# One VectorE instruction per pair of tiles for the moments, biases as a constant last column, one gelu per block, 23 squarings, and idle products of TensorE inside a planned schedule of an SSM, delta-rule and expert stack

## The chip, the cores and the metric

The kernel runs on one core of a Trainium2 chip. The metric is the device time of one launch in microseconds (us): 726.42 us, the median of 3 runs of the kernel before (725.71 to 728.25). All data is float32.

## What is computed

The input is `u`, 8 sequences of 512 steps with 128 features. Four layers follow each other; each normalises its input over the features (no gain, eps 1e-5) and adds its result to the stream. Cut to what matters:

```python
def layernorm(x):                              # m, v over the 128 features
    return (x - m) / sqrt(v + 1e-5)

# 1. gated scan. W_in and W_out (128x128) are divided by max(largest singular value, 1)
raw = u @ Wp.T + bp ;  delta, b, c = split(raw, 3)
a = min(exp(-softplus(delta + delta_bias) * alpha), 1 - 1e-4) ;  b, c = tanh(b), tanh(c)
...                                            # a, b, c divided by max(sigma of [[a,b],[0,c]], 1)
z[t+1] = a[t] * z[t] + b[t] * u_scaled[t]      # per feature, along the 512 steps
x = x + (c * z) @ Wout_n.T

# 2. one linear operation of 8, chosen once for all tokens
idx = argmax(log_softmax(logits) + gumbel)
x = x + layernorm(x) @ W[idx] + b[idx]

# 3. delta rule, 16 heads of 8 features, state S (8x8) per head and sequence
q, k, v, beta = split(layernorm2(layernorm(x)) @ w_qkvb + b_qkvb, 4) ;  k = k / |k| ;  beta = sigmoid(beta)
S = S + (beta * (v - S k)) outer k ;  o = S q  # per step
x = x + (layernorm(x) + o @ w_out + b_out)

# 4. top 2 of 8 experts, 128 -> 512 -> 128
p = softmax(xf @ w_router) ;  weights = the two largest of p
x = x + sum over the two experts of weight * (gelu(xf @ w1[e] + b1[e]) @ w2[e] + b2[e])
```

## The kernel before

**Tiles and stages.** The 4096 tokens are 32 tiles of 128 tokens: 16 time steps of the 8 sequences. Tiles come in 8 chunks of 4 (a chunk is `g` in the code), and chunks in groups of 4, 8, 8, 8 and 4 tiles for the experts. For a chunk, `scanned` does layer 1 (feature-major, 128 x 512), `ssm_out` and `linear` layer 1's output and layer 2, `delta_in` prepares queries, keys, values and the small 4 x 4 matrices of layer 3, `delta_rule` runs the recurrence, `route` chooses experts. When a group is complete, `experts` writes its token rows to a table in memory sorted by expert (indirect DMAs of POOL), runs the experts over blocks of 128 rows (15 blocks for 4 tiles, 23 for 8; 99 in all), and gathers the two results of each token back.

**The recurrence.** `delta_rule` goes through the 32 tiles in 4 blocks of 4 steps each: 128 blocks, each a chain of 6 VectorE operations. `so<-kq,st` multiplies keys and queries by the state, `st<-so` sums over the 9 terms, `prod<-tmat,st` and `st<-prod` solve the four steps of the block, `st<-kq,st` forms the state's terms and the second `st<-st` sums them into the next state. The state lives in two PSUM banks used in turn, `st[0]` (`st0`) and `st[1]`: columns 0 to 319 of each bank hold terms, the next 32 the sums `w`, and `st[1]` also holds `u_16`, the results of 16 steps, that ScalarE copies to `upd` once per tile. Columns 352 to 511 of `st[0]` aren't used. TensorE's other products use the banks `in`, `ph` and `po`, two each.

**Front work.** `spectral` finds the largest singular value of both weight matrices: `SQUARINGS + 1` = 25 products of the 128 x 128 matrix by itself, rescaled every third step by sums that TensorE, VectorE and ScalarE compute together; two such chains run interleaved, one per matrix, and end in `gain`, which `ssm_out` needs. `moments` takes for each tile one `bn_stats` and one `bn_aggr` of VectorE; `factors` makes from mean and variance a scale and a shift on POOL, `normalised` applies them on ScalarE. This is done four times in the stream, with the suffixes i, a, b and e.

**Experts.** `hidden_of` loads the weights of a block (`w1b`, 128 x 516 with the bias in the last 4 columns) from `w1b_dram`, a copy of the weights with biases that is made at the start. The row is chosen by a register. Four products fill `ph`, then four gelu instructions of 128 x 128 read it, each with its bias column, and `second` multiplies `hid` by `w_sb`. `linear` adds the chosen bias `bsel` to `x1` on POOL first.

**What sets the order.** Every call on an engine is recorded by `Recorder` in a `Plan` as an operation with a cost (`_cost`), a due time (`nc.key`) and its data dependences; a bank of PSUM may be chosen by the planner. `place` puts them on five engine timelines one after the other, by due time and by the earliest possible start. `best` tries `DRAFTS` = 60 drafts with changed due times and keeps the shortest. `emit` issues the operations in that order, so that each engine's queue has a fixed order. Waits between engines are derived from data and from PSUM banks afterwards. All recorded operations carry one source line, 317, in the profile (325 in the changed kernel), so groups are told apart by names and sizes.

Of the kernel before, what the change touches and what calls it, by code (L numbers as in the profile page):

```python
# [25 lines left out]
SQUARINGS = 24  # L26
# [44 lines left out]
class Plan:  # L71
# [112 lines left out]
    def best(self):  # L184
# [3 lines left out]
        for draft in range(DRAFTS):  # L188
# [10 lines left out]
            for turn in range(ROUNDS + 1):  # L199
# [4 lines left out]
                if kept is None or end < kept[0]:  # L204
                    kept = end, order, index, due, self.switch
        for bank, i in kept[2].items():
            bank.index = i
# [73 lines left out]
    def emit(self):  # L281
        kind = mybir.EngineType
        with self.tc.manual_schedule(engines={kind.PE, kind.DVE, kind.Activation, kind.SP}):
            for op, switch in self.best():
                if switch:
                    self.hw.scalar.preload_act_table_set(switch)  # L286
# [54 lines left out]
def _cost(engine, name, n, kw):  # L341

    if engine == "tensor":
        return 0.2 if name == "transpose" else 0.22 + 0.0019 * max(_size(kw["rhs"])[1] - 96, 0)
# [4 lines left out]
    if engine == "scalar":  # L349
        columns = sum(isinstance(kw.get(k), bass.AP) for k in ("bias", "scale"))  # L350
        return 0.18 + 0.00085 * n + (0.0, 0.0001 * n, 0.13)[columns]
    return 0.22 + 0.0015 * n if n < 64 else 0.4 + 0.0017 * n
# [5 lines left out]
DRAFTS = 60  # L358
# [3 lines left out]
LAG = {"tensor": 0.4, "vector": 0.3, "scalar": 0.3, "gpsimd": 0.3, "sync": 0.3}  # L362
SWITCH = (3.0, 6.0, 9.0, 12.0)
# [3 lines left out]
def seq_kernel(  # L367
# [93 lines left out]
    WIDE = {"both": 2 * N, "xne": P, "w1b": NHB * P + NHB, "drive": N + B, "z": N + B, "kq": NR * QN, "prod": B * BL * BL}  # L461
# [23 lines left out]
    def po_tile():  # L485
        return nc.bank(0, 1, 2)
# [20 lines left out]
    R_BP, R_AL, R_DB, R_G, R_B, R_QKVB, R_B1 = 0, 3, 4, 5, 6, 7, 11  # L507
    n_rows = R_B1 + NE * NHB
# [4 lines left out]
    nc.scalar.dma_start(rows[R_QKVB : R_QKVB + 4], b_qkvb.rearrange("(c p) -> c p", p=P))  # L513
    nc.scalar.dma_start(rows[R_B1:], b1.rearrange("e (c p) -> (e c) p", p=P))
# [12 lines left out]
    nc.sync.dma_start(wr, w_router)  # L527

# [88 lines left out]

    nc.vector.memset(st[0], 0.0)
# [33 lines left out]
    def col(r):  # L652
# [3 lines left out]
    FW = NHB * P + NHB  # L656
    w1b_dram = dram.tile([NE * P, FW], F32, tag="w1b_dram", name="w1b_dram")
    nc.key = 0.0
    nc.sync.dma_start(w1b_dram[:, 0 : NHB * P], w1.rearrange("e d f -> (e d) f"))
    nc.sync.dma_start(  # L660
        w1b_dram[:, NHB * P :].rearrange("(e p) c -> p e c", p=P),
        cols[:, R_B1:].rearrange("p (e c) -> p e c", c=NHB),
    )
# [41 lines left out]
    nc.vector.tensor_copy(w_row, pk[:, 4:5])  # L705
    b_row = ctile([P, 1], "b_row", U32)
    nc.vector.tensor_copy(b_row, topi[:, 0:1])
    wsel = ctile([P, D], "wsel")
    bsel = ctile([P, D], "bsel")
    for dst, src, row in (  # L710
        (wsel, ffn_W.rearrange("e d f -> (e d) f"), w_row),
        (bsel, ffn_b, b_row),
# [6 lines left out]
        )  # L719


    def moments(src, part, bufs=2):

        n = src.shape[1]
        st = stile([P, NT, 6], "st" + part)
# [851 lines left out]
```

## Time and profile before

| what | number |
|---|---|
| median of 3 runs | 726.42 us (725.71 to 728.25) |
| profiled execution, whole | 728.65 us |
| profiled execution, span of the trace | 726.9 us |
| granted TensorE clock, mean of the span | 0.832 |
| instructions | 11166 |
| TensorE (PE) busy | 520.2 us (72%) |
| VectorE (DVE) busy | 527.0 us (73%) |
| ScalarE (ACT) busy | 468.8 us (64%) |
| GpSimd (POOL) busy | 548.1 us (75%) |
| DMA moved | 105.94 MB, mean 146 GB/s |

The busy shares are means over the whole span, and no engine stands out in them; what limits a stage is read from its stretch. The profile's 40 slices give each engine's busy share in tenths, a slice being 18.2 us, and `PEclk` the clock that TensorE was granted in tenths of full speed. In TensorE's rows a float32 product appears as two records, so 792 records of `ph<-xbT,w1b` are the 396 products of 99 blocks. Groups name output and inputs by the program's names: `st` is one of the two state banks, `ph`, `in`, `po` the other banks.

### The profile page before, as it was taken

Reading aid. Unit: us, or ns where it says so; the run is one execution under the profiler, and the core shown is the slowest. Engines: PE = TensorE matmul, PEld = TensorE weight load, DVE = VectorE, ACT = ScalarE, POOL = GpSimd, SP = SyncE. Lnnn points to the kernel's source line nnn. Section 1 sums busy time; section 2 is a strip of 40 time slices with the busy share of each in tenths; the row PEclk is TensorE's granted clock in tenths of the full one; section 3 lists DMA queues with packets and bytes.
Section 4 is the critical chain, followed back from the end, with each engine's and each line's share of the span. In section 5 each row is a group of like instructions: output and inputs, shape, how many; then the busy total and the mean of one; then the engine's idle time right before and its main releaser. Section 6 shows DMA issues by size and latency. Waiting matters only on the chain. (4 is left out here: it accounts for less than half of the span.)

```text
span 726.9 us, 11166 instructions
## 1 busy us (share of the span) xinstructions
PE 520.2 (72%) x2948; PEld 403.9 (56%) x2948; DVE 527.0 (73%) x1468; ACT 468.8 (64%) x1062; POOL 548.1 (75%) x681
## 2 busy tenths in 40 slices
PE   5885466576584288699558788883978887988890
PEld 4672124435353156368326577662857776888890
DVE  5775068998999799999959999995798998230013
ACT  3865747654692679998675987852675743675560
POOL 6667485694768899699868998978478878876454
PEclk9856566877699599889758889996899999999995
DMA  3734263233352564276456456565686786569662
GB/s 106 200 108 123 60 148 79 73 95 88 78 125 75 143 178 125 76 181 179 127 148 162 111 138 169 163 173 135 168 211 184 201 245 194 171 192 276 168 176 80
DMA packets 97717, 105.94 MB, mean 146 GB/s; under 512 B 9100, under 2 KB 72535, under 8 KB 97655
## 3 DMA queue, kind: packets, MB, share of 16 engines
q1 hardware_dynamic: 92992, 96.66, 49.2%
q0 software_dynamic: 4160, 8.53, 4.0%
q8 instruction: 25, 0.41, 0.3%
q14 instruction: 38, 0.30, 0.1%
q10 hardware_dynamic: 502, 0.03, 0.0%
HBM read 81.26 MB, written 23.94 MB: 145 GB/s over the span
## 5 line engine op out<-in xcount | busy, mean ns | idle before, releaser
L317 ACT ACTIVATE hid<-ph,w1b 128x128 f32<-128x128 f32 x396 | 113.4, 378 | 48.7 <-PE ph L317 23.4
L317 PE MATMUL ph<-xbT,w1b 128*128 128x128 f32 x792 | 118.3, 292 | 12.0 <-DMA w1b<-w1b_dram 5.4
L317 PEld LDWEIGHTS ph<-xbT,w1b 128*128 128x128 f32 x792 | 107.3, 205 | 26.4 <-issue 10.7
L317 DVE TENSOR_TENSOR so<-kq,st 128x512 f32<-128x512 f32 x128 | 87.5, 684 | 15.6 <-PE in L317 7.9
L317 POOL DMA_INDIRECT back<-results,small_dest x64 | 62.8, 982 | 33.0 <-issue 14.0
L317 DVE TENSOR_REDUCE st<-so 128x32 f32<-128x288 f32 x128 | 84.1, 657 | 3.5
L1297 PE MATMUL po<-w_sb,hid 128*128 x536 | 80.3, 288 | 7.2 <-ACT hid L317 4.0
L1297 PEld LDWEIGHTS po<-w_sb,hid 128*128 128x128 f32 x536 | 73.2, 204 | 15.7 <-issue 7.3
L1235 POOL DMA_INDIRECT places<-xne,small_dest x64 | 64.3, 1004 | 18.8 <-issue 13.7
L286 ACT ACT_TABLE_LOAD x52 | 66.7, 1283 | 6.2 <-DMA hid<-in_L_ffn_b_dram 5.4
L317 PE MATMUL po<-wo,so 128*128 128x128 f32 x256 | 45.0, 330 | 32.9 <-DVE so L317 14.8
L317 DVE TENSOR_REDUCE st<-st 128x64 f32<-128x320 f32 x128 | 63.6, 497 | 4.0
L317 PEld LDWEIGHTS po<-wo,so 128*128 128x128 f32 x256 | 41.3, 240 | 43.2 <-DVE so L317 16.1
L317 PE MATMUL in<-b,head_ones 128*128 128x512 f32 x80 | 50.6, 721 | 11.3 <-DVE x L317 3.6
L317 DVE TENSOR_TENSOR st<-kq,st 128x256 f32<-128x256 f32 x128 | 54.8, 428 | 4.2
L317 PE MATMUL in<-f,wT 128*128 128x512 f32 x64 | 44.5, 789 | 15.1 <-ACT qkp L317 5.4
L317 POOL TENSOR_TENSOR qkp<-qkp,upd 128x512 f32<-128x512 f32 x32 | 38.8, 1214 | 13.3 <-ACT upd L317 13.2
L317 PE MATMUL in<-b,wqkvb 128*128 128x512 f32 x64 | 40.5, 731 | 9.4 <-ACT beta L317 4.3
L317 DVE TENSOR_REDUCE st<-prod 128x32 f32<-128x128 f32 x128 | 37.6, 293 | 12.0 <-ACT upd L317 6.8
L317 POOL TENSOR_TENSOR so<-so 128x512 f32<-128x512 f32 x24 | 30.5, 1271 | 17.8 <-DVE so L317 17.7
L317 DVE SCALAR_TENSOR_TENSOR fin<-back,small_weight,fin 128x128 f32<-128x128 f32 x16 | 5.3, 353 | 51.5 <-DMA back<-results,small_dest 50.8
L317 DVE TENSOR_TENSOR prod<-tmat,st 128x128 f32<-128x128 f32 x128 | 36.6, 286 | 8.0 <-POOL tmat L317 3.5
(292 smaller groups left out, 1310.4 us busy)
## 6 DMA issues: line engine op xcount, KB each, us to landing
kq<-scratch SPq DMA_DIRECT2D x64, 512.0 KB
w1b<-w1b_dram SPq DMA_DIRECT2D x99, 258.0 KB
xb<-places SPq DMA_DIRECT2D x21, 256.0 KB
results<-yb SPq DMA_DIRECT2D x21, 256.0 KB
places<-yb SPq DMA_DIRECT2D x2, 1472.0 KB
x<-in_L_attn_u_dram SPq DMA_DIRECT2D x32, 64.0 KB
w1b_dram<-in_L_ffn_w_dram SPq DMA_DIRECT2D x1, 2048.0 KB
scratch<-qn SPq DMA_DIRECT2D x8, 256.0 KB
```

Source lines behind the costliest of these rows:

```text
L286: self.hw.scalar.preload_act_table_set(switch)
L317: return method(*(on(x) for x in args), **{k: on(x) for k, x in kw.items()})
L1235: rows_out = hw.gpsimd.indirect_dma_start(out=table[0 : nblk * P, :], out_offset=bass.IndirectOffsetOnAxis(ap=at, axis=0), in_=src, in_off ...
L1297: return hw.tensor.matmul(out_.on(nc.banks), lhsT=src, rhs=w2_f[:, bass.ds(at + c * P, P)], start=(c == 0), stop=(c == NHB - 1),)
```

## The change

1. `moments` makes one `bn_stats` for each pair of tiles, over a view in which the elements of the two tiles alternate, so that its two sets of statistics (of even and of odd elements) are those of the two tiles. `bn_aggr` goes; `factors` divides count times variance by 128 itself.
2. Biases become a weight row. A normalised row sums to zero over its 128 features, so its last feature is minus the sum of the others. That last feature is replaced by 1.0, the weights have their last row subtracted from all rows, and the last row holds the bias. This is done for the chosen linear operation (a third indirect load, `wlast`, and two VectorE operations), the router (one POOL subtraction), and the experts' first weights. For these `fold_weights` loads `w1[e]` and its last row spread over 128 partitions, subtracts on POOL and writes the result to `w1b_dram`, for each of 8 experts; `b1` goes to row 127 of each expert. The POOL addition of `bsel` goes, and `w1b` has 512 columns.
3. A block's gelu is one ScalarE instruction of 128 x 512 without a bias column.
4. `SQUARINGS` is 23 instead of 24; the rescaling is squared by two multiplications inside one instruction rather than by an operation of its own; the closing sums are computed by a product with the first power.
5. The planner tries 150 drafts, and some costs are changed.
6. `emit` looks at TensorE's planned timeline. Where the planned gap ahead of an operation is over 1.0 us, it issues products whose result nobody reads, `int(0.6 * gap / 0.24)` of them, ahead of that operation: one column of `ident` as weights, `ident` (128 x 128) as the moving operand, one row of `st[0]`, columns 384 to 511, as the destination.

The diff, cut to its core:

```diff
@@ -23,7 +23,7 @@
 NHB = 4
-SQUARINGS = 24
+SQUARINGS = 23
 FIRST = 9
@@ -203,6 +203,7 @@
                     kept = end, order, index, due, self.switch
+                    self.times = {op: (op.start, op.end) for op, _ in order}
         for bank, i in kept[2].items():
@@ -279,9 +280,16 @@
     def emit(self):
-        kind = mybir.EngineType
+        kind, free = mybir.EngineType, None
         with self.tc.manual_schedule(engines={kind.PE, kind.DVE, kind.Activation, kind.SP}):
             for op, switch in self.best():
+                if op.engine == "tensor":
+                    start, end = self.times[op]
+                    if free is not None and start - free > GAP:
+                        for _ in range(int(FILL * (start - free) / FILLER)):
+                            self.filler()
+                    free = end
                 if switch:
@@ -341,7 +349,7 @@
     if engine == "tensor":
-        return 0.2 if name == "transpose" else 0.22 + 0.0019 * max(_size(kw["rhs"])[1] - 96, 0)
+        return 0.16 if name == "transpose" else 0.18 + 0.0017 * max(_size(kw["rhs"])[1] - 96, 0)
     if engine == "vector":
@@ -349,17 +357,20 @@
         return 0.18 + 0.00085 * n + (0.0, 0.0001 * n, 0.13)[columns]
+    if name == "memset":
+        return 0.15 + 0.0008 * n
     return 0.22 + 0.0015 * n if n < 64 else 0.4 + 0.0017 * n
...
 BEHIND = 8.0
-DRAFTS = 60
+DRAFTS = 150
 JITTER = 15
...
 LAG = {"tensor": 0.4, "vector": 0.3, "scalar": 0.3, "gpsimd": 0.3, "sync": 0.3}
+GAP, FILL, FILLER = 1.0, 0.6, 0.24
 SWITCH = (3.0, 6.0, 9.0, 12.0)
@@ -458,7 +469,7 @@
-    WIDE = {"both": 2 * N, "xne": P, "w1b": NHB * P + NHB, "drive": N + B, "z": N + B, "kq": NR * QN, "prod": B * BL * BL}
+    WIDE = {"both": 2 * N, "xne": P, "w1b": NHB * P, "drive": N + B, "z": N + B, "kq": NR * QN, "prod": B * BL * BL}
@@ -525,6 +535,9 @@
     nc.sync.dma_start(wr, w_router)
+    wr_last = ctile([P, NE], "wr_last")
+    nc.sync.dma_start(wr_last, w_router[D - 1].partition_broadcast(P))
+    nc.gpsimd.tensor_sub(wr, wr, wr_last)
@@ -615,6 +628,8 @@
+    junk = st[0][0:1, 512 - P : 512]
+    nc.filler = lambda: hw.tensor.matmul(junk, lhsT=ident[:, 0:1], rhs=ident, start=True, stop=True)
     nc.vector.memset(st[0], 0.0)
@@ -653,14 +668,21 @@
-    FW = NHB * P + NHB
+    FW = NHB * P
     w1b_dram = dram.tile([NE * P, FW], F32, tag="w1b_dram", name="w1b_dram")
     nc.key = 0.0
-    nc.sync.dma_start(w1b_dram[:, 0 : NHB * P], w1.rearrange("e d f -> (e d) f"))
-    nc.sync.dma_start(
-        w1b_dram[:, NHB * P :].rearrange("(e p) c -> p e c", p=P),
-        cols[:, R_B1:].rearrange("p (e c) -> p e c", c=NHB),
-    )
+    nc.sync.dma_start(w1b_dram.rearrange("(e p) f -> e p f", p=P)[:, D - 1, :], b1)
+    def fold_weights():
+        for e in range(NE):
+            nc.key = due(-3.0 + 0.8 * e)
+            w, last = ptile([P, FW], "w1b", 5), ptile([P, FW], "hid", 3)
+            nc.sync.dma_start(w, w1[e])
+            nc.sync.dma_start(last, w1[e, D - 1].partition_broadcast(P))
+            nc.gpsimd.tensor_sub(w, w, last)
+            nc.sync.dma_start(w1b_dram[e * P : (e + 1) * P - 1], w[0 : P - 1])
@@ -703,12 +725,16 @@
     nc.vector.tensor_copy(w_row, pk[:, 4:5])
+    last_row = ctile([P, 1], "last_row", U32)
+    nc.vector.tensor_scalar(last_row, pk[:, 3:4], float(D), D - 1.0, ALU.mult, ALU.add)
     b_row = ctile([P, 1], "b_row", U32)
...
     wsel = ctile([P, D], "wsel")
-    bsel = ctile([P, D], "bsel")
+    both_ = ptile([P, 2, D], "x3", 2)
+    wlast, bsel = both_[:, 0, :], both_[:, 1, :]
     for dst, src, row in (
         (wsel, ffn_W.rearrange("e d f -> (e d) f"), w_row),
+        (wlast, ffn_W.rearrange("e d f -> (e d) f"), last_row),
         (bsel, ffn_b, b_row),
@@ -717,39 +743,46 @@
         )
+    nc.vector.tensor_sub(wsel, wsel, wlast)
+    nc.vector.scalar_tensor_tensor(wsel, bsel, ident[:, P - 1 : P], wsel, ALU.mult, ALU.add)
...
         n = src.shape[1]
-        st = stile([P, NT, 6], "st" + part)
-        mv = stile([P, NT, 2], "mv" + part, F32, bufs)[:, 0:n]
-        for i in range(n):
-            nc.vector.bn_stats(st[:, i, :], src[:, i, :])
-            nc.vector.bn_aggr(mv[:, i, :], st[:, i, :])
+        mv = stile([P, NT, 3], "mv" + part, F32, bufs)[:, 0:n]
+        for i in range(0, n, 2):
+            nc.vector.bn_stats(
+                mv[:, i : i + 2].rearrange("p i s -> p (i s)"), src[:, i : i + 2, :].rearrange("p i d -> p d i")
+            )
         return mv
...
         rstd = stile([P, norms, NT], "rstd" + part, F32, bufs)[:, :, 0:n]
-        nc.gpsimd.tensor_scalar_add(rstd[:, 0], mv[:, :, 1], LN_EPS)
+        nc.gpsimd.tensor_scalar(rstd[:, 0], mv[:, :, 2], 1.0 / P, LN_EPS, ALU.mult, ALU.add)
         if norms == 2:
-            nc.gpsimd.tensor_scalar(rstd[:, 1], mv[:, :, 1], 1.0 + LN_EPS, LN_EPS * LN_EPS, ALU.mult, ALU.add)
+            nc.gpsimd.tensor_scalar(rstd[:, 1], mv[:, :, 2], (1.0 + LN_EPS) / P, LN_EPS * LN_EPS, ALU.mult, ALU.add)
         nc.gpsimd.tensor_tensor(rstd, rstd, mhalf[:, 0:norms, 0:n], ALU.pow)
         shift = stile([P, norms, NT], "shift" + part, F32, bufs)[:, :, 0:n]
-        nc.gpsimd.tensor_mul(shift, mv[:, :, 0].unsqueeze(1).to_broadcast([P, norms, n]), rstd)
+        nc.gpsimd.tensor_mul(shift, mv[:, :, 1].unsqueeze(1).to_broadcast([P, norms, n]), rstd)
         nc.gpsimd.tensor_scalar_mul(shift, shift, -1.0)
...
-    def normalised(src, rstd, shift, xn, norm=0):
+    def normalised(src, rstd, shift, xn, norm=0, width=D):
         for i in range(src.shape[1]):
             nc.scalar.activation(
-                xn[i], src[:, i, :], AF.Identity, bias=shift[:, norm, i : i + 1], scale=rstd[:, norm, i : i + 1]
+                xn[i][:, 0:width],
+                src[:, i, 0:width],
+                AF.Identity,
+                bias=shift[:, norm, i : i + 1],
+                scale=rstd[:, norm, i : i + 1],
             )
@@ -877,11 +910,11 @@
         xT = ptile([P, n * P], "f", FIRST)
-        nc.scalar.copy(xT, transposed(normalised(x1, rstd, shift, tiles_of(ptile([P, n, D], "f", FIRST)))))
-        x1b = ptile([P, n, D], "f", FIRST)
-        nc.gpsimd.tensor_add(x1b, x1, over_tiles(bsel, n))
+        xn = ptile([P, n, D], "f", FIRST)
+        nc.gpsimd.memset(xn[:, :, D - 1 : D], 1.0)
+        nc.scalar.copy(xT, transposed(normalised(x1, rstd, shift, tiles_of(xn), 0, D - 1)))
         x2 = ptile([P, n, D], "x2", 2)
-        nc.vector.tensor_add(x2, tokens_out(xT, wsel), x1b)
+        nc.vector.tensor_add(x2, tokens_out(xT, wsel), x1)
         return x2
@@ -1066,7 +1099,7 @@
         rstd, shift = statistics(x3, "e")
-        x3n = normalised(x3, rstd, shift, [ptile([P, D], "xne", MAXT) for _ in range(NT)])
+        x3n = normalised(x3, rstd, shift, [ptile([P, D], "xne", MAXT) for _ in range(NT)], 0, D - 1)
         x3T = ptile([P, N], "x3T")
@@ -1287,7 +1320,7 @@
-            nc.add("tensor", emit, [values], [("registers", last, j0)], 0.2 * m)
+            nc.add("tensor", emit, [values], [("registers", last, j0)], 0.05 * m)
@@ -1302,7 +1335,7 @@
-            nc.add("tensor", emit, [src, w2_sb, ("registers", last, j - j % 4)], [out_], 0.28)
+            nc.add("tensor", emit, [src, w2_sb, ("registers", last, j - j % 4)], [out_], 0.24)
@@ -1329,11 +1362,7 @@
                 )
-            for c in range(NHB):
-                cs = slice(c * P, (c + 1) * P)
-                nc.scalar.activation(
-                    hid[:, cs], ph[:, cs], AF.Gelu_apprx_tanh, bias=w1b[:, NHB * P + c : NHB * P + c + 1]
-                )
+            nc.scalar.activation(hid, ph, AF.Gelu_apprx_tanh)
             return hid
@@ -1402,7 +1431,7 @@
     sp = ctile([P, 24], "sp")
-    smax, rmax, rtr, sums, lam, sig = (sp[:, i : i + 2] for i in (0, 2, 6, 8, 12, 14))
+    smax, rmax, rtr, lam, sig = (sp[:, i : i + 2] for i in range(0, 10, 2))
     nc.vector.tensor_reduce(smax, w_both, AX.X, ALU.max, apply_absolute_value=True)
@@ -1425,42 +1454,41 @@
-        def total(x, y, column):
-            sums_ = part[:, 2 * column + i : 2 * column + i + 1]
-            if x is y:
-                nc.scalar.activation(junk, x, AF.Square, accum_out=sums_)
-            else:
-                nc.vector.tensor_mul(junk, x, y)
-                nc.vector.tensor_reduce(sums_, junk, AX.X, ALU.add)
+        def summed(column):
             at = ph_tile()[:, 0:1]
...
+        def squares(x):
+            nc.scalar.activation(junk, x, AF.Square, accum_out=part[:, i : i + 1])
+            return summed(0)
         cur, a0 = power(), ptile([P, P], f"back{i}")
         scaled(cur, w_both[:, i, :], rmax[:, c])
-        factor = None
         for step in range(SQUARINGS + 1):
-            bank = po_tile()
-            nc.tensor.matmul(bank[:, 0:P], lhsT=cur, rhs=cur, start=True, stop=True)
-            if step % 3 == 0 and step < SQUARINGS:
-                trace = total(cur, cur, 0)
-                nc.vector.tensor_scalar_max(rtr[:, c], trace, 1e-18)
+            bank = po_tile()[:, 0:P]
+            nc.tensor.matmul(bank, lhsT=cur, rhs=cur, start=True, stop=True)
+            if step % 3 == 0:
+                nc.vector.tensor_scalar_max(rtr[:, c], squares(cur), 1e-18)
                 nc.vector.reciprocal(rtr[:, c], rtr[:, c])
-                nc.vector.tensor_mul(rtr[:, c], rtr[:, c], rtr[:, c])
             cur = a0 if step == 0 else power()
             if step % 3 == 1:
-                scaled(cur, bank[:, 0:P], rtr[:, c])
+                nc.vector.tensor_scalar(cur, bank, rtr[:, c], rtr[:, c], ALU.mult, ALU.mult)
             else:
-                copied(cur, bank[:, 0:P])
+                copied(cur, bank)
             yield
-        nc.vector.tensor_copy(sums[:, c], total(cur, a0, 0))
-        nc.vector.tensor_scalar_max(rtr[:, c], total(cur, ident, 1), TINY)
+        bank = po_tile()[:, 0:P]
+        nc.tensor.matmul(bank, lhsT=a0, rhs=cur, start=True, stop=True)
+        nc.vector.tensor_scalar_max(rtr[:, c], squares(cur), TINY)
         nc.vector.reciprocal(rtr[:, c], rtr[:, c])
+        nc.vector.tensor_mul(a0, cur, bank)
+        nc.vector.tensor_reduce(part[:, 2 + i : 3 + i], a0, AX.X, ALU.add)
+        nc.vector.tensor_mul(lam[:, c], rtr[:, c], summed(1))
         yield
@@ -1470,7 +1498,8 @@
         pass
-    nc.vector.tensor_mul(lam, sums, rtr)
+    for x in [ptile([P, D], "xne", MAXT) for _ in range(MAXT)]:
+        nc.gpsimd.memset(x[:, D - 1 : D], 1.0)
     nc.gpsimd.tensor_tensor(sig, lam, half, ALU.pow)
@@ -1502,6 +1531,7 @@
+    fold_weights()
     x2s = {g: first_layers(g) for g in range(2)}
```

The one hunk left out drops the bias rows of `b1` from a table of small vectors.

More of the change, by code (lines that the diff above doesn't have):

```diff
@@ L505, in seq_kernel @@
     nc.sync.dma_start(wp_raw, Wp.rearrange("(c p) d -> p c d", p=P))
-    R_BP, R_AL, R_DB, R_G, R_B, R_QKVB, R_B1 = 0, 3, 4, 5, 6, 7, 11
-    n_rows = R_B1 + NE * NHB
+    R_BP, R_AL, R_DB, R_G, R_B, R_QKVB = 0, 3, 4, 5, 6, 7
+    n_rows = R_QKVB + 4
     rows = ptile([n_rows, P], "hid", 3)
@@ L512, in seq_kernel @@
         nc.scalar.dma_start(rows[r : r + 1], v.rearrange("(c p) -> c p", p=P))
-    nc.scalar.dma_start(rows[R_QKVB : R_QKVB + 4], b_qkvb.rearrange("(c p) -> c p", p=P))
-    nc.scalar.dma_start(rows[R_B1:], b1.rearrange("e (c p) -> (e c) p", p=P))
+    nc.scalar.dma_start(rows[R_QKVB:], b_qkvb.rearrange("(c p) -> c p", p=P))
     lg_col = ctile([P, 1], "lg_col")
```

## The prediction, made before the changed kernel had run

> **What bounds the kernel now.** I read the page first: the 40 slices (where each engine is busy), then the table of windows by stage, the timeline of VectorE inside one stage, the waits, and the order of instructions of both kernels (which has no times). The slices and the row of one pair of totals:
>
> ```profile
> DVE  5775068998999799999959999995798998230013
> PEclk9856566877699599889758889996899999999995
> ```
>
> One slice is 18.2 us. VectorE is at eight tenths and more from slice 6 to slice 33 (109 to 620 us), nearly idle in slices 34 to 37, where TensorE's row stands at 8 and 9. So there are three stages with three limits. The table of windows gives their sizes (columns: stretch, length, then busy time and count of PE, PEld, DVE, ACT, POOL, granted clock, DMA share, GB/s):
>
> ```profile
> 0.00:105.00 105.00, 71.79 (x227) 45.31 (x227) 54.42 (x226) 64.50 (x147) 68.19 (x103) 0.71 0.47 129
> 109.00:620.00 511.00, 366.82 (x2072) 281.36 (x2071) 450.81 (x1161) 348.68 (x740) 414.71 (x511) 0.85 0.54 144
> 620.00:708.00 88.00, 78.75 (x649) 76.09 (x647) 11.91 (x53) 55.47 (x177) 56.34 (x59) 0.96 0.68 197
> ```
>
> The middle stage is the recurrence: 128 blocks one after the other, six VectorE operations each. One block in VectorE's timeline (start, duration):
>
> ```profile
> 201.41 0.69 DVE L317 TENSOR_TENSOR so<-kq,st 128x512 f32<-128x512 f32 x1
> 202.13 0.66 DVE L317 TENSOR_REDUCE st<-so 128x32 f32<-128x288 f32 x1
> 202.82 0.29 DVE L317 TENSOR_TENSOR prod<-tmat,st 128x128 f32<-128x128 f32 x1
> 203.14 0.29 DVE L317 TENSOR_REDUCE st<-prod 128x32 f32<-128x128 f32 x1
> 203.47 0.43 DVE L317 TENSOR_TENSOR st<-kq,st 128x256 f32<-128x256 f32 x1
> 203.94 0.50 DVE L317 TENSOR_REDUCE st<-st 128x64 f32<-128x320 f32 x1
> 204.47 0.69 DVE L317 TENSOR_TENSOR so<-kq,st 128x512 f32<-128x512 f32 x1
> ```
>
> The next block starts 3.06 us after this one, with 0.03 us between operations: 128 x 2.85 = 364 us of the 511 are these six, about 88 us are other VectorE work put between blocks, and the list of waits of VectorE in this stretch adds up to only some 28 us (largest: one of 7.9 us for PE, two together 6.8 us for ACT). So in 109 to 620 us, whatever lengthens VectorE's queue, or makes it wait, lengthens the kernel by that much. The profiled execution took 728.65 us (span 726.9), 2.2 us above the median of 726.42; I sum against 728.65 and take the 2.2 us off at the end.
>
> **Moments.** Now every tile of 128 x 128 takes two VectorE instructions. Timeline:
>
> ```profile
> 71.79 0.26 DVE L317 BATCH_NORM_STATS2 small_stb<-x 128x6 f32<-128x128 f32 x1
> 72.08 0.18 DVE L317 BATCH_NORM_AGGREGATE small_mvb<-small_stb 128x2 f32<-128x6 f32 x1
> 72.18 0.26 DVE L317 BATCH_NORM_STATS2 small_stb<-x 128x6 f32<-128x128 f32 x1
> ```
>
> From one to the next, 72.18 - 71.79 = 0.39 us a tile. The change makes it one instruction of 256 elements per two tiles, reading elements alternately from the two tiles, 512 bytes apart. The trace has no such instruction. From below: 0.26 + 128 x 0.96 ns (the slope of the 128x512 and 128x128 rows, 0.69 and 0.29) = 0.40 us. From above: the page has a VectorE reduce that strides by 512 bytes, 288 elements in 657 ns, and one without, 320 in 497 ns: 2.28 against 1.55 ns an element, a factor 1.47, so 0.59 us. I take 0.55, nearest to the strided row. About 88 tiles lie in the recurrence: 88 x 0.395 - 44 x 0.55 = 34.8 - 24.2 = -10.6 us (-17 at 0.40, -9 at 0.59). [...]
>
> **Gelu, biases.** 396 ScalarE instructions of 128x128 (378 ns, 113.4 us) become 99 of 128x512; the copies of 128x512 on ScalarE take 592 ns, the activation of 128x512 with a bias column 689: about 99 x 0.65 = 64 us, 49 us less. ScalarE isn't the limit in the recurrence (348.68 of 511), so it pays only in waits: of the 28 us that VectorE waits, those for ACT, POOL and what hangs on them may go. I take -5 (0 to -15). POOL loses 8 adds of 128x512 (1.27 us) and gains 8 subtractions of that size in folding the weights, even. Folding adds 24 DMAs on SP's queue, some 6 MB, at the measured mean of 146 GB/s about 42 us of traffic, beside loads of the front and of the first blocks.
>
> **Front (0 to 105 us).** One squaring less of 25 steps in a chain that runs from 9 to 57 us: about 1.7 us; the tiny multiplications (16 x 472 ns, some 1.04 and 0.83) off it and a shorter end, 2 to 3 us more; part of this hides beside the first scan, whose product is read in the same place. Moments of the first chunk: 4 x 0.39 - 2 x 0.55 = 0.5 us twice. 67 fillers that wait for no VectorE work sit here: the clock of this stage is 0.71, and 0.50 in 66 to 100 us. A product of 512 columns takes 2.08 us there (79.74 us) and 1.12 us at full clock (102.85 us); five such are on the path, so up to 5 us. Against it stand the folding's POOL work and DMAs. I take -4 (range -10 to +6).
>
> **Fillers in the recurrence.** This is the part that decides. They write into a corner of the bank st0. The order of instructions of the changed kernel shows 362 products in 70 runs. In 54 of the runs the first filler waits for VectorE's last operation on st0, and VectorE's next operation on st0 then waits for the run's last filler. Before, recurrence operations wait for TensorE only for real data. In 28 runs (140 fillers) the two VectorE operations are next to each other or one short operation apart: 3.0 us of VectorE work lies between them in all. In 26 runs (130 fillers) 77.7 us lies between, 1.4 us or more in each. The others (16 runs, 92 fillers) have no waiting VectorE operation. The price of one filler: real f32 products of 128 x 128 come in two records each and 16 records take 1.79 us (625.51 to 627.30 us in TensorE's timeline), so 0.22 us each at full clock; 0.42 at half, by the 512-column rows. Handing over to TensorE and back takes up to 0.2 us (0.04 to 0.2 between the end of a product and the VectorE copy that waits). A run of N costs 0.2 + 0.22 N less the VectorE work between:
> - 28 close runs: 28 x 0.2 + 140 x 0.22 - 3.0 = +33.4 us (at half clock +61.4). The longest are 15 fillers in block 51 and 17 in block 127, with nothing between.
> - 26 wide runs: +0.7 us (at half clock +8.6).
> - TensorE is in order, so a run also waits until TensorE gets to it, and what is queued behind it is late by as much. In the trace of before TensorE and VectorE are mostly within 1 us of each other at the same point of the order; 26 waits of some 0.1 us, +3 (0 to +20).
>
> What it could buy, a clock above 0.85, helps TensorE, which here is not the limit. [...]
>
> **Tail (620 to 708 us).** TensorE is busy 78.75 of 88. Waits for w1b from memory are 5.4 us in 4 times; w1b buffers now come free at the last product of a block and not after its gelu. -4 (0 to -8). The bias columns no longer tie gelu to w1b.
>
> **The sum.** 728.65 - 4 (front) - 10.6 (moments) - 5 (waits) + 33.4 + 0.7 (stalls) + 3 (lateness) - 4 (tail) = 742.2; less 2.2 to the median: **740 us**, 1.9% slower.
>
> **Rivals.**
> - *The fillers are cheap or hidden, and the kernel is faster.* A filler loads one column of weights only; if it takes one record, 0.11 us, the close runs cost 28 x 0.2 + 140 x 0.11 - 3.0 = 18.0 us: about 724, the edge of no change. If the other edits reach their bounds (-10 front, -17 moments, -15 waits, -8 tail = -50) with my stalls: 728.65 - 50 + 37.1 - 2.2 = 713.5; both, 697. I price it at 714. It decides once stalls and lateness together stay under about 21 us, or the gains pass 39. For it: VectorE's other work falls by some 136 instructions in this stage, and a planner that fills freed places may remove waits. Against: 28 us of waits is all there is to remove.
> - *The clock is half in many runs.* Runs sit where TensorE was idle, and slices with 5 and 6 in the clock row show that the clock falls there. With half the fillers at 0.42: about 52 us of stalls, 758; with a lateness of 10: 765. All at half: 776.
> - *The fillers don't lift the front's clock and folding delays it:* front +6 in place of -4, 750.
>
> **Chances.** Forecast (732 to 748) 0.40; front delayed (750) 0.10; half clock (765) 0.13; faster side (714) 0.37, of which 0.07 fall within 0.3% of before. About 0.3% (2.2 us) is what a measurement of this kernel can tell from no change. So faster 0.30, same 0.07, slower 0.63. The range 706 to 770 leaves out the corner of the faster side where both helps meet (0.10) and all runs at half clock (0.07).
>
> **What would show it.** In the profile after: groups of `st0` products on PE, VectorE's list of waits with "st <- PE st" or "so <- PE st" near 34 us where before had none; st0-writing gaps of 3 to 4 us at blocks 51 and 127; a BATCH_NORM_STATS2 group of 128x256 with a mean near 0.55 us; ScalarE's gelu x99 near 0.65 us; the clock of 66 to 100 us above 0.5. I am wrong if the waits for these products are under 20 us, if the recurrence gets shorter than 511 us, or if the other work of VectorE falls by more than 17 us.

## The result, and the profile after

The changed kernel takes **802.69 us** (median of 4 runs, 800.7 to 803.21) against 727.34 us for the kernel before in the same set of runs: a ratio of 1.103 (95% interval 1.0995 to 1.1066), 75 us slower. The direction was as forecast, the size not: 740 us was forecast, with a range to 770.

Read in the same order as before. First the slices of the page of the changed kernel (a slice is now 20.0 us):

```profile
DVE  5552022368877889878976899797787995522012
PEclk9769677589997899979977999898977999799895
GB/s 106 159 112 221 50 51 101 101 61 103 105 56 76 152 95 134 189 126 93 137 126 89 150 188 155 141 159 193 99 97 199 231 210 227 94 223 212 201 197 80
```

Two things differ from before. VectorE's row falls to 2, 0, 2, 2 in slices 3 to 6 (60 to 140 us, counted from 0 as before), where the kernel before has one such slice, and the memory moves only 50 GB/s in slices 4 and 5. In the busy part that follows there are sevens where there were nines. The windows put sizes to it (columns as before):

```profile
0.00:152.00 152.00, 82.72 (x375) 52.90 (x375) 48.44 (x164) 74.88 (x162) 83.34 (x129) 0.76 0.41 116
152.00:701.00 549.00, 429.70 (x2663) 314.02 (x2664) 444.26 (x1037) 298.44 (x528) 404.46 (x507) 0.88 0.50 135
```

Measured at three marks of VectorE's timeline (first `st<-so`, last `so<-kq,st`, end of the span), the 73.6 us between the two spans (726.9 and 800.5) fall like this:

| stage | before | after | difference | forecast |
|---|---|---|---|---|
| start to the first `st<-so` | 110.0 | 152.5 | +42.4 | -4 |
| from there to the last `so<-kq,st` | 506.9 | 544.9 | +38.1 | +21.5 |
| from there to the end | 110.0 | 103.1 | -6.9 | -4 |

(21.5 is -10.6 - 5 + 33.4 + 0.7 + 3 of the forecast's sum.) So two errors, and the larger is in the stage where I had booked a gain.

VectorE's list of waits in the recurrence (us in total, times, longest):

```profile
DVE st L325 <- PE st L632: 41.4, 24, 6.7
DVE so L325 <- DMA kq<-scratch: 25.3, 1, 25.3
DVE so L325 <- PE in L325: 12.8, 2, 8.5
DVE prod L325 <- PE st L632: 7.2, 5, 2.5
DVE x L325 <- PE in L325: 7.1, 2, 6.6
DVE so L325 <- PE st L632: 2.7, 4, 1.4
```

`PE st L632` are the fillers: 41.4 + 7.2 + 2.7 = 51.3 us in 33 waits, where the forecast had 34.1 plus 3. The second line is the first operation of the recurrence: its keys come from memory 25.3 us after VectorE is ready for them.

**Where the front goes.** VectorE's wait for `drive` in the changed kernel, the same wait in the kernel before, and POOL's timeline after the change:

```profile
DVE drive L325 <- POOL f L325: 27.9, 1, 27.9
```

```profile
DVE drive L317 <- POOL f L317: 19.9, 1, 19.9
```

```profile
79.16 2.49 POOL L325 TENSOR_TENSOR w1b<-w1b,hid 128x512 f32<-128x512 f32 x2
100.29 1.26 POOL L325 TENSOR_TENSOR w1b<-w1b,hid 128x512 f32<-128x512 f32 x1 [18.63 <-DMA w1b<-in_L_ffn_w_dram]
101.51 1.26 POOL L325 TENSOR_TENSOR f<-f,f 128x512 f32<-128x512 f32 x1
```

A subtraction that folds an expert's weights stands in POOL's queue and waits 18.6 us for its load; the `f<-f,f` of the second chunk is queued behind it, and VectorE's `drive` waits for that. But `drive` waited 19.9 us in the kernel before too, so this path adds 8 us; the 25.3 us of the late keys are the larger part of the 42.4. SP's queue carries those keys as well as the folding's loads and writes. Its list of waits, 60 to 152 us, names what holds it:

```profile
SPq L325 <- DMA w1b_dram<-w1b: 16.8, 3, 8.8
SPq L325 <- POOL w1b L325: 13.8, 2, 9.2
SPq L325 <- DMA scratch<-qn: 6.8, 1, 6.8
```

The first line is the write-back of the folded weights. The DMA view of 113 to 133 us (40 slices of half a microsecond) shows how fast that goes:

```profile
GB/s 25 29 25 25 25 29 25 41 25 29 25 25 25 29 25 57 25 29 25 25 25 29 74 172 380 350 134 25 25 29 25 25 25 29 25 25 25 29 20 22
...
w1b_dram<-w1b SPq DMA_DIRECT2D x2, 254.0 KB
```

25 GB/s, stretch after stretch, but 380 in between: the memory can do more, and one slow transfer is running. In 128 to 131 us, at 25 GB/s, the mean busy share of the 16 DMA engines is 0.06, about what one of the 16 makes. 254 KB at 26 GB/s are 10 us, eight of them 80 us. 254 KB are 127 rows. That the row count is the reason is what the experiments have to show.

### The profile page after: what moved, and what is told of

Its sections match the earlier page's. It is cut to its first block, busy times and chain, and to the rows that moved or that the text cites. A ratio compares the mean times of both kernels' runs of the same rounds, so it can differ in the third digit from the quotient of the medians.

```text
span 800.5 us, 12151 instructions
## 1 busy us (share of the span) xinstructions
PE 588.3 (73%) x3672; PEld 440.3 (55%) x3672; DVE 511.4 (64%) x1265; ACT 408.7 (51%) x753; POOL 548.5 (69%) x699
## 4 chain that ended last, share of the span: by engine, by line
DVE 37%; PE 31%; DMA 11%; POOL 8%; issue 5%; ACT 3%; SPq 3%; POOLq 0%; DVEq 0%; ACTq 0%
DVE st L325 20%; PE st L632 10%; PE ph L325 7%; DVE so L325 6%; PE in L325 6%; PE po L1330 5%; DVE prod L325 3%; PE po L325 3%; SPq L325 3%; DMA hid<-in_L_ffn_w_dram 2%; DMA w1b_dram<-w1b 2%; POOL places L1268 2%; DMA scratch<-kn 1%; POOL b L325 1%; ACT f L325 1%
## 5 line engine op out<-in xcount | busy, mean ns | idle before, releaser
L632 PE MATMUL st<-ident 128*1 128x128 f32 x724 | 113.5, 316 | 107.0 <-DVE st L325 70.2
L632 PEld LDWEIGHTS st<-ident 128*1 128x1 f32 x724 | 63.1, 94 | 167.7 <-DVE st L325 87.8
L325 DVE TENSOR_TENSOR so<-kq,st 128x512 f32<-128x512 f32 x128 | 87.7, 685 | 46.2 <-DMA kq<-scratch 25.3
L325 PE MATMUL ph<-xbT,w1b 128*128 128x128 f32 x792 | 110.8, 286 | 0.7 <-ACT xbT L325 0.5
L325 PEld LDWEIGHTS ph<-xbT,w1b 128*128 128x128 f32 x792 | 101.7, 200 | 9.0 <-issue 4.4
L325 ACT ACTIVATE hid<-ph 128x512 f32<-128x512 f32 x99 | 58.4, 597 | 81.1 <-PE ph L325 75.7
L1330 PE MATMUL po<-w_sb,hid 128*128 x672 | 91.9, 282 | 2.8 <-ACT upd L325 2.5
L1330 PEld LDWEIGHTS po<-w_sb,hid 128*128 128x128 f32 x672 | 85.1, 198 | 9.3 <-issue 5.4
L325 PE MATMUL in<-b,wqkvb 128*128 128x512 f32 x64 | 37.0, 670 | 17.6 <-DVE drive L325 16.4
L325 POOL TENSOR_TENSOR f<-f,f 128x512 f32<-128x512 f32 x24 | 30.5, 1271 | 16.2 <-ACT f L325 16.2
L325 PE MATMUL in<-f,wT 128*128 128x512 f32 x64 | 38.7, 692 | 0.7 <-ACT f L325 0.7
```

Of the source, the lines that this page charges most:

```text
L325: return method(*(on(x) for x in args), **{k: on(x) for k, x in kw.items()})
L632: nc.filler = lambda: hw.tensor.matmul(junk, lhsT=ident[:, 0:1], rhs=ident, start=True, stop=True)
L1330: return hw.tensor.matmul(out_.on(nc.banks), lhsT=src, rhs=w2_f[:, bass.ds(at + c * P, P)], start=(c == 0), stop=(c == NHB - 1),)
```

## The experiments

Each theory below is about one of the two: the 127-row writes (front) and the fillers in `st0` (recurrence); then what is left of the gain. Ratios are to runs of the kernel before on the same chip, whose medians were 729.6 to 730.1 us.

### Without fillers

```diff
-GAP, FILL, FILLER = 1.0, 0.6, 0.24
+GAP, FILL, FILLER = 1.0, 0.0, 0.24
```

> The changed kernel with FILL 0: the same planned order, and no product that nobody reads. VectorE's list of waits in the changed kernel has 51.3 us in 33 waits for the products into st0. Theory (the fillers cost what that list says, because nothing else is late underneath): the recurrence gets shorter by 45 to 51 us, VectorE waits for TensorE in it only for real products, and the start of the recurrence stays near 152 us, since its delay has another cause: 802.7 - 48 = about 755 us. Rival (under each filler run VectorE's work was waiting for something else anyway): under 20 us are gained, over 782 us, and other waits stand in the list instead. Second rival (TensorE's clock falls back without the fillers, and the front gets longer): start of the recurrence later than 157 us.

Measured: 751.76 us (747.17 to 753.16), ratio to before 1.0284 (1.0236 to 1.0332). 50.9 us less than the changed kernel. The stage from the first `st<-so` to the last `so` is 496.9 us, 48.0 less, and it starts at 153.9, hardly changed. So 48.0 of the 51.3 us in the list of waits come back in that stage: little else was late under the fillers, and both rivals fall.

### 128 rows written back

```diff
-            nc.sync.dma_start(w1b_dram[e * P : (e + 1) * P - 1], w[0 : P - 1])
+            nc.sync.dma_start(w1b_dram[e * P : (e + 1) * P], w)
```

> The changed kernel with one edit: the eight folded weights are written back with 128 rows in place of 127 (row 127 of the difference is zero, which is what b1 is here, so b1 itself is left out). The planned order of all engines is the same. In the changed kernel the DMAs move 24 to 27 GB/s in most slices from 82 to 145 us. Theory (127 rows put a write on a single DMA engine, some 254 KB at 26 GB/s = 10 us each, and everything behind it on SP's queue waits, keys of the first blocks included): writes take 1 to 2 us, the recurrence starts at 105 to 115 us in place of 151.7, total about 762 us. Rival (it is the amount of loads and the eight subtractions on POOL, whatever the row count): start stays after 140 us, total above 790 us.

Measured: 752.55 us (747.31 to 753.35), ratio 1.0298 (1.0244 to 1.0353), 50.1 us less than the changed kernel, from one row more, and some 10 us more of a gain than expected. The recurrence starts at 104.9 us in place of 151.7. The same loads and subtractions are there, so the rival falls. Its DMA view of 60 to 105 us:

```profile
DMA packets 10837, 10.02 MB, mean 223 GB/s; under 512 B 431, under 2 KB 8495, under 8 KB 10833
```

10.02 MB in 45 us; the changed kernel took from 60 to 152 us for 10.09 MB.

### Both

> Both edits of the two runs before at once (b1 left out, zero here). If the two costs are independent, 802.7 - 48 - 40 = about 715 us, faster than the 727 of before; by my sum on record, which has 23.6 us of gains without stalls, 703. If one hides the other, above 725 us.

Measured: 708.46 us (707.56 to 711.97), ratio 0.9722 (0.9679 to 0.9766). The costs add up nearly: alone they give 50.9 and 50.1, together 94.2, so 7 us are counted twice. What is left is a kernel 2.8% faster than before, between the two values expected (715, and 703 by the sum on record without stalls and lateness: 728.65 - 23.6 - 2.2 = 702.9).

### Which row counts are slow

Without fillers; the weights of seven experts are written in two parts, each split at another row, and those of the eighth at once. The question is whether 127 rows alone are slow or every count but 128.

```diff
-            nc.sync.dma_start(w1b_dram[e * P : (e + 1) * P - 1], w[0 : P - 1])
+            n = (127, 126, 124, 120, 112, 96, 64, 128)[e]
+            nc.sync.dma_start(w1b_dram[e * P : e * P + n], w[0:n])
+            if n < P:
+                nc.sync.dma_start(w1b_dram[e * P + n : (e + 1) * P], w[n:P])
```

> No fillers; each of the eight folded weights is written in two parts: 127+1, 126+2, 124+4, 120+8, 112+16, 96+32, 64+64 rows and 128 at once. [...] Rival (every write that isn't of 128 rows is slow): all first parts but the last show 26 GB/s and some 10 us. [...]

A single execution: 700.77 us; the recurrence starts at 108.7 us. (The second part's last row overwrites b1, zero here.) The DMA view of 41 to 60 us, in which the 127 rows are written:

```profile
GB/s 276 293 306 293 289 280 293 311 371 160 52 26 69 78 60 39 190 207 250 259 194 69 22 26 26 26 26 26 26 26 26 26 26 26 22 0 306 246 172 250
```

The stretch at 26 GB/s appears once, from 51.5 to 57 us, while that write has nothing beside it. The 126 rows are issued in the same view, at some 48 us, and show no second such stretch. From 72 to 86 us, with 124 rows and the counts below it, the slices show 70 to 390 GB/s apart from two empty ones, and again no such stretch:

```profile
GB/s 149 171 142 135 102 187 212 192 165 208 181 252 146 152 88 111 105 181 252 293 363 252 258 345 334 193 70 88 187 316 392 392 240 246 217 211 76 0 0 246
```

So the rival falls: not every odd shape is slow; 127 is, at 26 GB/s. Why that count is slow the run doesn't show, and it doesn't separate the other counts from each other.

### The fillers alone, in the kernel before

> The kernel before with the fillers alone, in its own planned order: 293 products in 55 runs; 61 of them stand ahead of the recurrence; 37 runs lie between two VectorE operations on st0. By the formula on record these cost 27 us at full clock; the changed kernel's list had 51 us where the formula gave 34, so times 1.5 it is 41. Theory (a filler run couples the two engines at its full price): 727 + 27 to 41 = 754 to 768 us. Rival (fillers lift the clock and pay for themselves): 720 to 730 us. Rival (the price in the changed kernel comes from its new order): under 740 us.

The edit is those lines of the diff above that make the fillers (`self.times`, `emit`, `GAP`, `junk` and `nc.filler`), in the kernel before. Measured: 761.71 us (761.24 to 763.75), ratio 1.0439 (1.0404 to 1.0475), +32 us. The recurrence is 540.6 us in place of 506.9. Its list of waits:

```profile
DVE st L325 <- PE st L628: 37.3, 14, 5.0
...
DVE prod L325 <- PE st L628: 6.3, 3, 4.1
...
DVE so L325 <- PE st L628: 1.4, 1, 1.4
```

45.0 us in 18 waits, where the formula gave 27, so it is too low here as in the changed kernel. The recurrence grew by 33.7 us only: VectorE's other waits in it fell from 28.6 to 18.5 us, so some 10 us were waited for anyway. The mean clock rose from 0.832 to 0.880, and the kernel got slower all the same. Both rivals fall, also the one that the price belongs to the new order.

### Only runs of fewer than eight

```diff
-                        for _ in range(int(FILL * (start - free) / FILLER)):
+                        n = int(FILL * (start - free) / FILLER)
+                        for _ in range(n if n < 8 else 0):
                             self.filler()
```

> The changed kernel with 128 rows (b1 left out, zero here) and only the filler runs of fewer than 8 products; same planned order. In the run with all fillers VectorE's gaps that end with a filler run in the recurrence were 22.6 us for the 11 runs of 8 and more, 28.7 for the shorter ones. Theory (each run costs what its gap shows): 752.5 - 22.6 = 730 us, so the short runs alone cost 22 to 29 us over the 708.5 without. Rival (short runs hide, the long ones that run at half the clock are the price): 715 us or less. Second rival (the long runs lift the clock for the short ones): short runs then cost up to 0.42 us a product, 740 us or more.

Measured, with 128 rows: 738.76 us (737.51 to 744.65), ratio 1.0141 (1.0091 to 1.0192). The short runs cost 30.3 us over the 708.46 without any, just above the 22 to 29 expected; without the long ones 13.8 us are gained, and not 22.6. The waits of the short runs are 32.4 us here (19.7 + 9.0 + 3.7), more than the 28.7 they had beside the long ones. So long and short runs aren't additive; both cost, and the rival that short runs hide falls. The second rival is right in part. The 46 short runs of the recurrence take 58.6 us of TensorE's timeline here and 51.0 in the run with 128 rows and all fillers; 19 of them are slower than 0.33 us a product here, 9 there. So some short runs do go slower without the long ones, and the waits that end with short runs are 3.7 us longer. The rest of the missing 8.8 us (22.6 - 13.8) stays open.

### Fillers ahead of the recurrence only

Fillers until the first operation of the recurrence, and the writes as 112 and 15 rows (the lines for the writes are left out here).

```diff
-                    if free is not None and start - free > GAP:
+                    if not begun and free is not None and start - free > GAP:
...
                 made = op.emit()
+                begun = begun or op.key[1] == self.first
```

> The changed kernel in its planned order, with two edits: a folded weight is written back as 112 and 15 rows instead of 127 (b1 stays in), and fillers are issued only until the first operation of the recurrence (67 products in 12 runs). The run with 128 rows and all fillers started the recurrence at 104.9 us, the one with 128 rows and none at 110.1: theory (ahead of the recurrence nobody waits for the fillers and the clock is higher): start near 105 us, and the rest as without fillers: 708.5 - 5 = 703 us. Rival (what the front gains is lost again in a later wait, as the recurrence waits for chunk 2 anyway): 707 us or more.

Measured: 708.88 us (703.8 to 711.81), against 708.46 (707.56 to 711.97) without fillers: the median is on the rival's side, but the runs spread over both. Windows of 60 to 105 us, the run without fillers and with 128 rows first, then this one:

```profile
60.00:105.00 45.00, 24.86 (x62) 11.84 (x61) 11.86 (x26) 30.37 (x51) 38.64 (x64) 0.61 0.70 205
```

```profile
60.00:105.00 45.00, 36.59 (x193) 19.62 (x192) 15.49 (x30) 33.70 (x57) 42.37 (x69) 0.92 0.78 224
```

The clock does rise, from 0.61 to 0.92, and this profile starts the recurrence at 106.1 in place of 110.1 us. But the run with four gelu instructions (below), with no filler and the same order, starts at 105.8 us at a clock of 0.73; its first gelu comes at 263 us. The total shows no gain; whether the front's 4 us are real and lost later stays open.

### One bn_stats and one bn_aggr per tile again

In the place of each instruction for a pair, in the order of the run without fillers and with 128 rows.

```diff
-            nc.vector.bn_stats(
-                mv[:, i : i + 2].rearrange("p i s -> p (i s)"), src[:, i : i + 2, :].rearrange("p i d -> p d i")
-            )
+            def emit(i=i):
+                for j in range(i, i + 2):
+                    hw.vector.bn_stats(st6[:, j, :], src[:, j, :])
+                    made = hw.vector.bn_aggr(mv[:, j, 1:3], st6[:, j, :])
+                return made
...
```

> The run without fillers and with 128 rows (b1 left out, zero here), with one bn_stats and one bn_aggr per tile put back in the place of each instruction for a pair; same planned order. In the changed profile a pair's instruction takes 0.42 us and the next follows after 0.385 us; two tiles took 2 x 0.395 before. Theory (VectorE is the bound of the recurrence): 42 pairs x (0.79 - 0.385) = 17 us longer, 725 us. Rival (the shorter moments only lengthened VectorE's other waits): under 716 us.

Measured: 730.73 us (724.53 to 733.07, 10 runs), ratio to before 0.9997 (0.9969 to 1.0024): 22 us more than without the edit. Between the two profiled executions, which differ by 18.5 us, the recurrence grows from 494.0 to 511.6 us, 17.6 as expected. With this edit the whole gain of the version without fillers and with 128 rows over the kernel before is gone.

### Four gelu instructions again

> The run without fillers and with 128 rows (b1 left out, zero here), with four gelu instructions of 128x128 (no bias column) in the place of each of 128x512; same planned order. ScalarE gets 99 x (4 x 0.36 - 0.60) = 83 us more work. Theory (ScalarE isn't the bound of any stage): under 4 us longer, up to 712 us. Rival (the recurrence waits for upd and others from ScalarE, and TensorE in the tail for hid): 8 to 25 us longer, 716 us or more.

Measured: 712.38 us (706.98 to 715.1) against 708.46, ratio to before 0.9749 (0.969 to 0.9808). Some 4 us, at the edge of the theory and within the spread; the rival's 716 isn't reached. The expected 83 us more work was wrong: a gelu of 128x128 without a bias column takes 291 ns, with it 378 (before). 396 of them keep ScalarE busy for 76.8 us, 99 of 128x512 (597 ns) for 58.4, so the merging saves 18 us and the bias column, at 113.4 before, 37. The difference in the mean of one is 87 ns.

### The planner's costs and drafts of before

> The run without fillers and with 128 rows (b1 left out, zero here), with the planner's costs and its 60 drafts as in the kernel before; the operations are the same, their order isn't. Theory (the gain of 21 us over the kernel before comes from VectorE's shorter work, not from the new order): 702 to 715 us. Rival (the planner's changes carry it): 718 us or more.

Measured: 708.31 us (705.59 to 709.02). No difference in the total: the planner's new costs and drafts don't carry the gain.

### The moments alone, in the kernel before

> The kernel before with the moments in one instruction per pair of tiles and nothing else; the planner finds its own order for it. Putting them back cost 22 us in the changed kernel. Theory (the moments are nearly the whole gain): 706 to 712 us. Rival (they pay only together with the other edits): 716 us or more.

Measured: 721.04 us (719.11 to 722.37), ratio 0.9869 (0.9839 to 0.99): 9 us, not 20. The theory fails, and the total is what the rival forecast. VectorE's list of waits from 112 to 620 us in this kernel:

```profile
DVE prod L317 <- POOL tmat L317: 10.4, 2, 9.7
DVE so L317 <- issue: 8.7, 3, 5.0
...
DVE st L317 <- ACT upd L317: 6.6, 1, 6.6
```

The instructions are as short (423 to 426 ns on `x`), but VectorE now waits 10.4 us for `tmat` of POOL where before had 3.5, and 8.7 us for nothing that the profile shows ("issue"). By the three marks the recurrence is 498.9 us, 7.9 shorter and not 17.6; the front is 8.8 shorter and the rest after the last `so` 9.3 longer than before. Which of the other edits takes the waits away wasn't separated, and the planner's order is another one here.

### The changed kernel without the two costs

```diff
-            nc.sync.dma_start(w1b_dram[e * P : (e + 1) * P - 1], w[0 : P - 1])
+            nc.sync.dma_start(w1b_dram[e * P : e * P + 112], w[0:112])
+            nc.sync.dma_start(w1b_dram[e * P + 112 : (e + 1) * P - 1], w[112 : P - 1])
...
-GAP, FILL, FILLER = 1.0, 0.6, 0.24
+GAP, FILL, FILLER = 1.0, 0.0, 0.24
```

> The changed kernel without fillers, its folded weights written as 112 and 15 rows (b1 stays in), in the planner's own order for these operations, which is that of the run with the row counts. That one took 700.8 us in one look, with one write of 127 rows still in it. Theory (all that was lost is the fillers and the 127 rows): 696 to 704 us, faster than both kernels. Rival (the one look was a lucky one, as runs of one order spread over some 8 us): 705 to 712 us.

Measured: **701.82 us** (698.27 to 703.14), ratio to before 0.9595 (0.9558 to 0.9632). This is the fastest version, 4% below before and 101 us below the changed kernel, and it still writes `b1`. As a test of the two costs it isn't clean: in the changed kernel's own order the version without both takes 708.46 us (128 rows), and 708.88 with 112 and 15 rows and the fillers of the front. So some 6.6 us of the gain come with the other order of operations, and that the total meets the 703 of the sum on record is in part luck.

## Why the prediction was wrong

**The front: -4 forecast, +42.4 measured. This is the step that failed.** The prediction counted folding as "some 6 MB, at the measured mean of 146 GB/s about 42 us of traffic, beside loads" and gave it no term of its own; the third rival names the delay, but prices it at +6 for the front and 750 in all. A mean over all queues is no price for one transfer: the write has 127 rows and moves at 26 GB/s, and the 24 DMAs are in order with the keys of the first blocks on SP, the subtractions in order with the scan's products on POOL. What an operation that waits in a queue does to those behind it was priced for the fillers and not for the fold. One row more takes 50.1 us off. The upper bound of the front (+6) had no basis in any row, and the range missed for that reason. What the front's other edits gain can't be told from the spread: with 128 rows the first `st<-so` starts at 105.6 us with all fillers and at 110.8 without, against 110.0 before.

**The fillers: 34.1 + 3 forecast, 51.3 us of waits and 50.9 us of time measured** (44.1 with 128 rows). The mechanism was right (bank `st0`, two-way waits, long runs with nothing between); the term of the price was too small. In PE's timeline of the changed kernel:

```profile
62.57 4.31 PE L632 MATMUL st<-ident 128*1 128x128 f32 x38
...
73.26 2.78 PE L632 MATMUL st<-ident 128*1 128x128 f32 x24
```

19 products in 4.31 us are 0.23 us each, as forecast, ahead of the recurrence. Inside it two runs look like this:

```profile
357.06 6.30 PE L632 MATMUL st<-ident 128*1 128x128 f32 x30 [6.06 <-DVE so L325]
363.30 0.66 PE L325 MATMUL in<-ident,b 128*128 128x128 f32 x4
```

```profile
688.38 6.63 PE L632 MATMUL st<-ident 128*1 128x128 f32 x34 [6.98 <-DVE so L325]
```

15 products in 6.30 us, 0.42 each, and VectorE's `st<-so` after them waited 6.40 us, where the forecast had 3.5 (6.5 at half clock). The run waits for VectorE before it can begin, so TensorE has been idle for 6 to 7 us (6.06 and 6.98), and the run meets the lowered clock that it was to prevent. Two windows show it, one ahead of the gap and one of the first run's first half (the clock is the third number from the end, 1.00 and then 0.50; the first half of the second run, 688.4 to 691.7 us, has 0.50 too):

```profile
345.00:350.90 5.90, 5.61 (x41) 4.49 (x39) 5.39 (x13) 5.83 (x9) 3.65 (x6) 1.00 0.50 147
357.06:360.40 3.34, 3.33 (x16) 2.01 (x17) 0.00 (x0) 0.15 (x1) 1.75 (x2) 0.50 0.32 98
```

Of the 57 runs in the recurrence 16 (some 115 products) went at over 0.33 us a product from start to end, and 29.3 of the 51 us of waits end with them. The rival at half clock named this with 52 us of stalls; I gave it 0.13. Runs of up to seven fillers go with a higher clock too: with only those, the mean clock is 0.859 against 0.821 without any, and 0.86 against 0.84 in the recurrence (both with 128 rows). It bought no time.

**Moments: -10.6 forecast, -17.6 measured in the recurrence.** One instruction takes 0.42 us, and the next starts 0.34 us after it (120.34 and 120.68 below, then 121.02, in the run without fillers and with 128 rows), less than the lower bound of 0.40 and far from the strided row. The factor 1.47 that the reduce shows doesn't appear here: 128x256 with alternate elements 512 bytes apart takes 425 ns, 128x128 contiguous 270. (The slope of the two rows that the lower bound names is 1.04 ns an element and not 0.96; the bound of 0.40 stands by it. The expectation with 0.385 from one to the next had that figure too high.)

```profile
L325 DVE BATCH_NORM_STATS2 small_mvb<-x 128x6 f32<-128x256 f32 x16 | 6.3, 425 | 0.2
```

```profile
120.34 0.42 DVE L325 BATCH_NORM_STATS2 small_mvb<-x 128x6 f32<-128x256 f32 x1
...
120.68 0.41 DVE L325 BATCH_NORM_STATS2 small_mvb<-x 128x6 f32<-128x256 f32 x1
```

**Waits: -5 forecast, -1.2 measured.** Without fillers and with 128 rows VectorE's list of waits in the recurrence adds up to 27.4 us, against 28.6 before. The recurrence is 494.0 us, 12.9 under before and not 17.6 + 1.2: some 6 us more of VectorE's other time lie in it than before, which wasn't traced further.

**Tail: -4 forecast, -6.9 measured** (-7.8 with 128 rows and without fillers). Right in sign and within its range of 0 to -8; no run separates its cause.

**The rival on the faster side** (fillers absorbed) was wrong in every form; the sum without stalls and lateness, 703, is about what the versions without both costs reach (701.8 to 708.5).

**The signs.** None of the three signs of being wrong came true: the waits were over 20 us, the recurrence got longer, and VectorE's busy time fell by 15.6 us. All three looked at VectorE's chain and the fillers, none at the front. The reading of the slices was too smooth as well: in slices 6 to 33 VectorE's row has two sevens and two fives.

## What to carry to other kernels

Price each DMA that a change adds by its own shape, and ask who stands behind it in its queue; a mean bandwidth hides a transfer of 127 rows at 26 GB/s. In this kernel a product that nobody reads still held the bank it was written to: 33 waits of VectorE's chain ended with such runs, 51.3 us in all, and a run of 15 that began after 6.06 us without work of TensorE took 0.42 us a product, its first half at a granted clock of 0.50. When an edit on the bounding engine pays 22 us in one version and 9 in another, look at which waits grew.

## What the runs showed of the hardware beyond this

Some versions spread further than the kernel before: 703.8 to 711.8 us with fillers ahead of the recurrence, 706.98 to 715.1 with four gelus, against 728.54 to 732.45 for the kernel before on the same chip. Two profiles of one order without fillers (with one gelu and with four, whose first comes at 263 us) differ in the front's clock (0.61 and 0.73 in 60 to 105 us) and in the start of the recurrence (110.1 and 105.8 us), so a difference of a few microseconds there can't be put down to an edit.

A filler that writes to a bank which the recurrence doesn't use wasn't tried, so how much of the fillers' price is the shared bank and how much TensorE's time is not shown: the kernel's other banks (`in`, `ph`, `po`, two each, beside `st[1]`) are all in use, and the order of the products in them would change with it.
